# Layer 1: softplus summed on TensorE, 3x3 convolution on four 64x64 tiles; one output row per token in the mixture of experts

## The chip, the cores and the metric

One core of a Trainium2 chip runs the whole program. The time is the device time in microseconds (us), as the median of ten runs. Engines are named as in the profile: PE is TensorE, DVE is VectorE, ACT is ScalarE, POOL is GpSimd, SP is SyncE (it only issues DMAs here).

## The reference, cut to what matters

Input `x` is 32 images of 128 channels, 56x56, f32. Two layers follow each other.

Layer 0, a convolution block with a mixture of experts:

```python
x = conv7x7_depthwise(input); x = layernorm(x)           # T = 32*56*56 tokens of 128 values
topv, topi = top_k(x @ Wg, 2); wts = softmax(topv)       # two of E = 8 experts for each token
# each expert takes at most cap = 1.25*T/E tokens
h = gelu(einsum('ecd,edf->ecf', eb, W1) + b1)
y = einsum('ecf,efd->ecd', h, W2) + b2
moe = sum over the two experts of (gate * y)
return input + x + layer_scale * moe
```

Layer 1, a Mamba block beside a 3x3 depthwise convolution:

```python
xh = cv1_w @ x
l  = silu(batchnorm(conv3x3_depthwise(xh)))
t  = layernorm(xh)                                        # tokens in raster order
xm, z = split(t @ in_proj_w.T)                            # 256 channels each
xm = silu(causal_conv1d(xm, 4 taps))
dt, Bm, Cm = split(xm @ x_proj_w.T)
dt = softplus(dt @ dt_proj_w.T + dt_proj_b)
h_t = exp(dt_t * A) * h_(t-1) + dt_t * Bm_t * xm_t        # 16 states for each channel
y   = einsum(h_t, Cm_t) + xm * D
g   = (y * silu(z)) @ out_proj_w.T
out = x + cv2_w @ concat([l, g])
```

## The kernel before

The program runs in four stages, one after the other.

**Convolution** (to about 2000 us). The 7x7 depthwise convolution runs on PE; the normed tokens go to the DRAM tensor `res_d`, which has 2T rows of 128 values. Rows 0 to T-1 hold the tokens, rows T to 2T-1 are filled with zeros by 14 DMAs of 3584 KB (line 246). **Routing and dispatch** (to about 5025 us). DVE ranks the tokens; then POOL issues 1792 indirect DMAs that scatter token rows into `buf_d`, sorted by expert (line 404). Each row carries its gate and the index of the row of `res_d` that its result is to be added to: token t for the first choice of expert, T + t for the second (`backs`). **Experts** (to about 7054 us). For each expert, 35 groups of up to four tiles of 112 rows are loaded, multiplied on PE, and added to `res_d` by indirect DMAs with an add (`products`, line 455; 1120 of them, issued by POOL). `apart(inst, group)` declares that the DMAs of one group name don't depend on each other; all of them have the name "back".

**Layer 1** (to the end). A group is 8 rows of one image, 448 tokens; there are 32 x 7 = 224 groups, and each takes 16 steps, one for each state. The loop at the end of `layer1` writes the order of every engine's instructions out by hand (`manual_schedule`). Step t works on unit t, that is state i = t mod 16 of group g. In each step:

- ACT copies the last state of unit t-1 (`carry_act`, line 966), then computes exp(dt*A) of unit t+1 into the PSUM tile `da` (`exp_act`, two instructions, line 945; two `da` tiles).
- DVE does the scan of unit t (`scan_dve`, line 954) and the product with C (`cmul`, line 960). For the states 0, 3, 7, 11 and 14 (`POOL_C`) POOL does that product instead, a step later.
- POOL computes dt*B*xm of unit t+4 (`db_pool`, line 939).
- In odd steps PE adds the products of two units into the PSUM tile `py` (`sum_pe`, through `tiles`: four matmuls on the four 64x64 quarters of the array, line 902).
- Last come the side works, which the calls `at(offset, function)` put at step 16*g + offset: they prepare a later group or finish an earlier one. `yz_dve` alone comes ahead of the scan of its step.

In what follows "step 7" means all steps with t mod 16 = 7. Before the change the side works stand so: 14 `moe_act`; 6 `cv1_pe`; 7 `cv1_act`; 8 `var_pe`; 9 `rstd_act`; 10 `rstd_pool`; 11 `bc_pe`; 12 `te_dve`; 15 and 0 `xm_pe`; 1 `silus` (a table load, SiLU of the two halves of xm, of lt and of the two halves of z, with the z matmuls issued inside, and a table load back); 2 `px_pe`; 3 `px_act`; 4 `dt_pe`; 5 to 10 the softplus; 10 and 11 `lt_pe` (the 3x3 convolution: 9 matmuls with diagonal 128x128 weights); 12 `lt_act`; 2 `yz_dve`; 3 `out_pe`; 4 `out_act`; 13 `moe_pe` (two matmuls for each of four tiles, one for each half of `res_d`).

The softplus is computed as relu(v) + (ln(u) - ((u - 1) - e)) with e = exp(-|v|) and u = 1 + e. ACT does abs, relu, exp, the add of 1 and the logarithm; DVE does `sp_r` (line 856) and `sp_add` (line 868), POOL does `sp_sub` (line 864), each on 128x896 values.

All side works of PE share two PSUM banks through `mm_tile`: a new tile waits until the tile before the last one has been read.

Of the kernel before, what the change touches and what calls it, by code (L numbers as in the profile page):

```python
# [5 lines left out]
F32 = mybir.dt.float32  # L6
I32 = mybir.dt.int32
AF = mybir.ActivationFunctionType
ALU = mybir.AluOpType
# [34 lines left out]
def tile_kernel(tc: tile.TileContext, a: dict, out: bass.AP):  # L44
# [11 lines left out]
    with (  # L56
# [5 lines left out]

        res_d = dram.tile([2 * T, C], F32, name="res_d")


        zero = const.tile([TT, 1, RW], F32, name="zero")
        nc.gpsimd.memset(zero, 0.0)
        nc.gpsimd.memset(zero[:, :, C + 1].bitcast(I32), 2 * T)
        ident = const.tile([128, 128], F32, name="ident")
# [172 lines left out]
        for k in range(0, E * CAP // TT, 80):  # L242
            nc.sync.dma_start(out=buf_t[:, k : k + 80, :], in_=zero.to_broadcast([TT, 80, RW]))
        res_t = res_d.rearrange("(k p) c -> p k c", p=TT)
        for k in range(COLS, 2 * COLS, 64):
            nc.sync.dma_start(out=res_t[:, k : k + 64, :], in_=zero[:, :, :C].to_broadcast([TT, 64, C]))

# [140 lines left out]
        with tc.tile_pool(name="dispc", bufs=1) as dc, tc.tile_pool(name="disp", bufs=3) as dp:  # L388
            backs = []
            for k in range(2):  # L390
                bi = dc.tile([TT, COLS], I32, name=f"bi{k}")
                nc.gpsimd.iota(bi, pattern=[[TT, COLS]], base=k * T, channel_multiplier=1)
                backs.append(bi)
            for n in range(N):
                cols = slice(n * TPI, (n + 1) * TPI)
                for k in range(2):
                    xg = dp.tile([TT, TPI, RW], F32, name=f"xg{k}")
                    nc.sync.dma_start(
                        out=xg[:, :, :C], in_=res_d[n * L : (n + 1) * L, :].rearrange("(k p) c -> p k c", p=TT)
                    )  # L400
                    nc.vector.tensor_copy(xg[:, :, C], gates[k][:, cols])  # L401
                    nc.vector.tensor_copy(xg[:, :, C + 1].bitcast(I32), backs[k][:, cols])
                    for j in range(TPI):
                        apart(nc.gpsimd.indirect_dma_start(  # L404
                            out=buf_d[:, :],
                            out_offset=bass.IndirectOffsetOnAxis(
                                ap=slots[k][:, n * TPI + j : n * TPI + j + 1], axis=0
                            ),
                            in_=xg[:, j, :], in_offset=None, bounds_check=ZR - 1, oob_is_err=False,
                        ), "scatter")  # L410
# [4 lines left out]
        with (  # L415
# [12 lines left out]

            def products(g, xb, xc, w1t, w2t, b1t, b2t):

# [21 lines left out]
                )  # L452

                for j in range(g):
                    apart(nc.gpsimd.indirect_dma_start(  # L455
                        out=res_d[:, :],
                        out_offset=bass.IndirectOffsetOnAxis(ap=xb[:, j, C + 1 : C + 2].bitcast(I32), axis=0),
                        in_=ys[:, j, :], in_offset=None, bounds_check=2 * T - 1, oob_is_err=False, compute_op=ALU.add,
                    ), "back")

            for e in range(E):
# [10 lines left out]
                for i0 in range(0, ntile, GT):  # L472
# [11 lines left out]
                    if todo:  # L484
                        products(*todo.pop())
                    todo.append((g, xb, xc, w1t, w2t, b1t, b2t))
            products(*todo.pop())


        with (  # L490
# [36 lines left out]
            nc.vector.tensor_tensor(bbi, bbi, bsc, ALU.mult)  # L527
            nc.vector.tensor_tensor(bbi, bnb, bbi, ALU.subtract)

            wk = wp.tile([C, DC, DI], F32, name="wk")  # L530
# [99 lines left out]
def layer1(s):  # L630
# [5 lines left out]
    mm_tile, res_d, x_d, out_d = s["mm_tile"], s["res_d"], s["x_d"], s["out_d"]  # L636
    perm, T = s["perm"], s["T"]
    G = N * NQ1
# [4 lines left out]
    with (  # L643
# [23 lines left out]
        def fetch(g):  # L667
            n, q = divmod(g, NQ1)
            d = st[g]
            t0 = n * L + q * CH1  # L670
            d["x1"] = three.tile([C, CH1], F32, name="x1", bufs=5)
            nc.sync.dma_start(out=d["x1"], in_=x_d[n, :, q * CH1 : (q + 1) * CH1])
            d["yg"] = two.tile([TT, TPC1, 2, C], F32, name="yg")
            for k in range(2):
                r = k * T + t0
                nc.sync.dma_start(
                    out=d["yg"][:, :, k, :], in_=res_d[r : r + CH1, :].rearrange("(j p) c -> p j c", p=TT)
                )

        def moe_pe(g):  # L680
# [4 lines left out]
            for j in range(TPC1):  # L685
                for k in range(2):
                    nc.tensor.matmul(
                        p[:, j * TT : (j + 1) * TT], lhsT=yg[:, j, k, :], rhs=perm,
                        start=False, stop=k == 1 and j == TPC1 - 1,
                    )  # L690

# [144 lines left out]


        def sp_abs(g):
            d = st[g]
# [13 lines left out]

        def sp_r(g):
            d = st[g]
            nc.vector.scalar_tensor_tensor(d["e"], d["u"], 1.0, d["e"], ALU.subtract, ALU.subtract)

        def sp_ln(g):
            d = st[g]
            nc.scalar.activation(d["u"], d["u"], AF.Ln)  # L860

        def sp_sub(g):
            d = st[g]
            nc.gpsimd.tensor_tensor(d["u"], d["u"], d.pop("e"), ALU.subtract)

        def sp_add(g):
            d = st[g]
            nc.vector.tensor_tensor(d["dt"][:, :, 1:], d["dt"][:, :, 1:], d.pop("u"), ALU.add)

# [4 lines left out]

        def lt_pe(g, ts):
            d = st[g]
            if ts[0] == 0:
                d["p_l"] = mm_tile("p_l")
            for t in ts:
                dy, dx = divmod(t, 3)  # L880
                nc.tensor.matmul(  # L881
                    d["p_l"][:, :CH1], lhsT=s["dwd"][:, t, :], rhs=d["xh"][:, dy : dy + ROWS1, dx : dx + HW],
                    start=t == 0, stop=t == 8,
                )

        def lt_act(g):
            d = st[g]
            d["lt"] = two.tile([C, CH1], F32, name="lt")
            nc.scalar.activation(d["lt"], d.pop("p_l")[:, :CH1], AF.Identity, bias=s["bbi"], scale=s["bsc"])

# [89 lines left out]
        at(18, yz_dve)  # L980
        at(19, out_pe)
        at(20, out_act)
        at(-35, moe_pe)
# [5 lines left out]
        at(-22, rstd_pool)  # L989
        at(-21, bc_pe)  # L990
        at(-20, te_dve)
        at(-17, xm_pe, 0)
        at(-16, xm_pe, 1)
        at(-15, silus)
        at(-14, px_pe)
        at(-13, px_act)
        at(-12, dt_pe)
        at(-11, sp_abs)
        at(-10, sp_exp)
        at(-9, sp_r)  # L1000
        at(-8, sp_ln)
        at(-7, sp_sub)
        at(-6, sp_add)
        at(-5, du_pool)
        at(-6, lt_pe, range(0, 5))
        at(-5, lt_pe, range(5, 9))
        at(-4, lt_act)
        work.setdefault(DS * G - 15, []).append((silus, G))

# [76 lines left out]
```

## Time and profile before

| what | value |
|---|---|
| median of 10 runs | 18460.58 us (18454.04 to 18467.01) |
| the profiled execution | 18468.28 us, span 18466.6 us |
| convolution stage, to about | 2000 us |
| routing and dispatch, to about | 5025 us |
| experts, to about | 7054 us |
| layer 1 | 7054 us to the end |
| one group of layer 1 (scan of step 8 to the next: 12111.80 to 12162.29 us) | 50.49 us |

The profile's timeline gives for each instruction its start, its duration, the engine, the line of the kernel, the operation with output and inputs, and in brackets the idle time before it with what ended that. The duration of one instruction overlaps the next one on its engine by about 0.1 us, so sums along an engine are made with the distances of starts. One f32 matmul appears as two instructions (two passes), and so does its weight load.

### The profile page before, as it was taken

To read this page: it belongs to the slowest core of one execution; us is meant where nothing else is said; L and a number is where in the kernel's file an instruction comes from. 1 tells how busy PE (TensorE), PEld (TensorE's weight loads), DVE (VectorE), ACT (ScalarE), POOL (GpSimd) and SP (SyncE) were. 2 spreads that over 40 slices of the span, in tenths; PEclk is the share of its full clock that TensorE was granted. 3 is DMA by queue.
4 is the path that set the end of the run, shared out by engine and by line. 5 is a ranking of instruction groups with operands and counts; after the bars stand their busy time and mean duration, and the time that the engine had idled before them with its cause. 6 is when DMAs were issued, how large, how long until landed. Compare 5 with 4: busy or idle time off the path is not lost. (4 is left out here: it accounts for less than half of the span.)

```text
span 18466.6 us, 214770 instructions
## 1 busy us (share of the span) xinstructions
PE 13649.9 (74%) x75528; PEld 7238.3 (39%) x75528; DVE 12453.7 (67%) x9487; ACT 9674.8 (52%) x18556; POOL 14869.9 (81%) x9599
## 2 busy tenths in 40 slices
PE   4887110000099998888888888888888888888888
PEld 4887100000077774333333333333333333333333
DVE  1766730000011116999999999999999999999999
ACT  2333000000044445777777777777777777777776
POOL 1333036666688888999999999999999999999999
PEclk8997555555599999999999999999999999999999
DMA  9779622222255554555555555555555555555555
GB/s 224 205 208 203 146 57 66 66 68 68 52 67 68 68 67 118 166 166 165 166 164 165 165 164 165 166 165 165 166 164 164 165 165 165 166 166 166 165 165 155
DMA packets 1761563, 2633.97 MB, mean 143 GB/s; under 512 B 149674, under 2 KB 1220441, under 8 KB 1756385
## 3 DMA queue, kind: packets, MB, share of 16 engines
q1 hardware_dynamic: 1554656, 2464.60, 46.4%
q0 software_dynamic: 205824, 155.64, 5.9%
q8 instruction: 595, 9.75, 0.2%
q14 instruction: 488, 3.99, 0.1%
HBM read 2231.69 MB, written 426.81 MB: 144 GB/s over the span
## 5 line engine op out<-in xcount | busy, mean ns | idle before, releaser
L939 POOL TENSOR_TENSOR db<-du,bb 128x896 f32<-128x896 f32 x3584 | 7423.5, 2095 | 0.1
L954 DVE TENSOR_TENSOR_SCAN da<-da,db 128x898 f32<-128x898 f32 x2464 | 4978.2, 2020 | 86.8 <-ACT da L945 86.6
L945 ACT ACTIVATE da<-dt,aneg 128x449 f32<-128x449 f32 x7168 | 4578.4, 639 | 587.7 <-DVE hs L954 243.5
L902 PE MATMUL py<-prod,ident 64*64 64x448 f32 x28672 | 3475.1, 599 | 115.5 <-POOL prod L960 103.6
L960 DVE TENSOR_TENSOR prod<-da,cb 128x896 f32<-128x896 f32 x2464 | 2689.3, 1091 | 197.4 <-issue 4.4
L960 POOL TENSOR_TENSOR prod<-hs,cb 128x896 f32<-128x896 f32 x1120 | 2323.9, 2075 | 382.8 <-issue 329.6
L954 DVE TENSOR_TENSOR_SCAN hs<-da,db 128x898 f32<-128x898 f32 x1120 | 2262.1, 2020 | 246.7 <-ACT db L966 209.7
L404 POOL DMA_INDIRECT buf_d<-xg,slot x1792 | 1686.6, 941 | 816.5 <-issue 807.5
L481 PE MATMUL ept<-ident,xb 112*128 112x112 f32 x1120 | 200.0, 260 | 2530.9 <-DMA xb<-buf_d 2530.9
L483 ACT COPY xc<-ept 128x448 f32<-128x448 f32 x280 | 149.1, 532 | 3508.3 <-DMA xb<-buf_d 2531.0
L455 POOL DMA_INDIRECT res_d<-ys,xb x1120 | 1652.1, 1475 | 374.0 <-issue 323.4
L881 PE MATMUL p_l<-xh,dwd 128*128 128x448 f32 x4032 | 1745.9, 580 | 0.0
L902 PEld LDWEIGHTS py<-prod,ident 64*64 64x64 f32 x28672 | 982.7, 141 | 1942.2 <-issue 1115.6
L401 DVE COPY xg<-gate 112x28 f32<-112x28 f32 x64 | 13.5, 227 | 2252.6 <-DMA buf_d<-xg,slot 2252.5
L776 PE MATMUL p_xm<-te,wk 128*128 128x448 f32 x3584 | 1415.8, 546 | 0.0
L447 DVE TENSOR_TENSOR ys<-py,b2t 112x512 f32<-112x512 f32 x280 | 193.6, 691 | 1533.5 <-PE py L442 1525.9
L881 PEld LDWEIGHTS p_l<-xh,dwd 128*128 128x128 f32 x4032 | 793.4, 207 | 959.4 <-issue 958.0
L481 PEld LDWEIGHTS ept<-ident,xb 112*128 112x128 f32 x1120 | 137.5, 142 | 2532.0 <-issue 2531.8
L442 PEld LDWEIGHTS py<-w2t,hh 128*112 128x112 f32 x8960 | 1031.1, 177 | 163.4 <-issue 115.8
L442 PE MATMUL py<-w2t,hh 128*112 128x128 f32 x8960 | 1094.9, 275 | 0.0
L174 PE MATMUL pc<-xc,toep 112*112 112x112 f32 (+1 forms) x8192 | 980.3, 279 | 107.0 <-ACT toep L163 66.0
L203 POOL TENSOR_TENSOR xa<-xa,lng 112x896 f32<-112x896 f32 x128 | 278.6, 2176 | 955.2 <-DVE xa L200 602.6
(222 smaller groups left out, 19781.7 us busy)
## 6 DMA issues: line engine op xcount, KB each, us to landing
bb<-bc_d SPq DMA_DIRECT2D x1792, 448.0 KB
cb<-bc_d SPq DMA_DIRECT2D x1792, 448.0 KB
toep<-toep_d SPq DMA_DIRECT2D x448, 392.0 KB
xg<-res_d SPq DMA_DIRECT2D x64, 1568.0 KB
yg<-res_d SPq DMA_DIRECT2D x448, 224.0 KB
buf_d<-zero SPq DMA_DIRECT2D x14, 4550.0 KB
xb<-buf_d SPq DMA_DIRECT2D x280, 227.5 KB
xt<-in_x SPq DMA_DIRECT2D x32, 1568.0 KB
```

Source lines behind the costliest of these rows:

```text
L174: nc.tensor.matmul(pc[:, c, :, lo:hi], lhsT=tp[c // 2][:, c % 2, 6 - 2 * o : 8 - 2 * o, :], rhs=s4[:, c, :, lo + o - 1 : hi + o - 1], star ...
L404: apart(nc.gpsimd.indirect_dma_start(out=buf_d[:, :], out_offset=bass.IndirectOffsetOnAxis(ap=slots[k][:, n * TPI + j : n * TPI + j + 1], ...
L442: nc.tensor.matmul(py[:, j, :], lhsT=hh[:, k, j * TT : (j + 1) * TT], rhs=w2t[:, k, :], start=k == 0, stop=k == KF - 1,)
L455: apart(nc.gpsimd.indirect_dma_start(out=res_d[:, :], out_offset=bass.IndirectOffsetOnAxis(ap=xb[:, j, C + 1 : C + 2].bitcast(I32), axis=0 ...
L481: nc.tensor.transpose(pt[:, j * TT : (j + 1) * TT], xb[:, j, :C], ident[:TT, :TT])
L776: nc.tensor.matmul(p[:, :CH1], lhsT=s["wk"][:, k, hs], rhs=d["te"][:, k : k + CH1], start=k == 0, stop=k == DC - 1 and not first,)
L881: nc.tensor.matmul(d["p_l"][:, :CH1], lhsT=s["dwd"][:, t, :], rhs=d["xh"][:, dy : dy + ROWS1, dx : dx + HW], start=t == 0, stop=t == 8,)
L902: nc.tensor.matmul(st[g]["py"][h * HD : (h + 1) * HD, r, :CH1], lhsT=lhsT(rs, h), rhs=rhs[rs, h, :], start=start, stop=stop,)
L939: nc.gpsimd.tensor_tensor(dbv[i][:, :, 1:], st[g]["du"], units[u].pop("bb"), ALU.mult)
L945: nc.scalar.activation(da[:, h * W1 : (h + 1) * W1], st[g]["dt"][:, h, :], AF.Exp, scale=s["aneg"][:, h, i : i + 1])
L954: nc.vector.tensor_tensor_scan(hs, da, dbs[i], 0.0, ALU.mult, ALU.add)
L960: eng.tensor_tensor(w["prod"], w["hs"][:, :, 1:], w.pop("cb"), ALU.mult)
```

## The change

Four things change.

1. Both experts of a token add to the same row of `res_d`, which now has T rows: the 14 zero-fill DMAs go, the index of a row is t for both choices, and in layer 1 one DMA fetches a group's rows instead of two, with four matmuls instead of eight in `moe_pe`. The indirect DMAs of an expert have a group name of their own, so those of one expert wait for those of the experts before it.
2. The three elementwise steps of the softplus on DVE and POOL go. ACT now also subtracts 1 from u, four matmuls for each half (with the identity, or minus the identity for u - 1) add the four terms in PSUM, and ACT copies the two halves to `dt`.
3. The 3x3 convolution runs on the four 64x64 quarters of PE's array, as `sum_pe` does: a diagonal 128x128 weight needs only its two diagonal 64x64 blocks. For each tap there are four matmuls on 64 channels and 224 columns, into two PSUM tiles, and `lt_act` reads the result with four instructions on 64 x 224 values.
4. Most side works of layer 1 move by one or two steps.

```diff
-        res_d = dram.tile([2 * T, C], F32, name="res_d")
+        res_d = dram.tile([T, C], F32, name="res_d")
...
-        for k in range(COLS, 2 * COLS, 64):
-            nc.sync.dma_start(out=res_t[:, k : k + 64, :], in_=zero[:, :, :C].to_broadcast([TT, 64, C]))
...
-                    ), "back")
+                    ), f"back{e}")
...
+            bnt = wp.tile([128, 2, 2], F32, name="bnt")
+            for k in range(2):
+                for r in range(2):
+                    for j, v in enumerate((bbi, bsc)):
+                        nc.scalar.copy(bnt[k * HD : (k + 1) * HD, r, j : j + 1], v[r * HD : (r + 1) * HD, :])
+            negi = wp.tile([128, 128], F32, name="negi")
+            nc.vector.tensor_scalar_mul(negi, ident, -1.0)
...
-            for k in range(2):
-                r = k * T + t0
-                nc.sync.dma_start(
-                    out=d["yg"][:, :, k, :], in_=res_d[r : r + CH1, :].rearrange("(j p) c -> p j c", p=TT)
-                )
+            nc.sync.dma_start(
+                out=d["yg"], in_=res_d[t0 : t0 + CH1, :].rearrange("(j p) c -> p j c", p=TT)
+            )
...
-        def sp_r(g):
-            nc.vector.scalar_tensor_tensor(d["e"], d["u"], 1.0, d["e"], ALU.subtract, ALU.subtract)
         def sp_ln(g):
-            nc.scalar.activation(d["u"], d["u"], AF.Ln)
-        def sp_sub(g):
-            nc.gpsimd.tensor_tensor(d["u"], d["u"], d.pop("e"), ALU.subtract)
-        def sp_add(g):
-            nc.vector.tensor_tensor(d["dt"][:, :, 1:], d["dt"][:, :, 1:], d.pop("u"), ALU.add)
+            d["l"] = one.tile([128, 2, CH1], F32, name="sp_l")
+            nc.scalar.activation(d["l"], d["u"], AF.Ln)
+            nc.scalar.add(d["u"], d["u"], -1.0)
+        def sp_pe(g, h):
+            d[f"p_sp{h}"] = p = mm_tile("p_sp")
+            terms = ((s["negi"], d["u"]), (ident, d["e"]), (ident, d["l"]), (ident, d["dt"][:, :, 1:]))
+            for k, (w, v) in enumerate(terms):
+                nc.tensor.matmul(p[:, :CH1], lhsT=w, rhs=v[:, h, :], start=k == 0, stop=k == 3)
+        def sp_act(g, h):
+            nc.scalar.copy(d["dt"][:, h, 1:], d.pop(f"p_sp{h}")[:, :CH1])
...
         def lt_pe(g, ts):
-                d["p_l"] = mm_tile("p_l")
+                d["p_l"] = [mm_tile("p_l") for r in range(2)]
+            R = ROWS1 // 2
             for t in ts:
                 dy, dx = divmod(t, 3)
-                nc.tensor.matmul(
-                    d["p_l"][:, :CH1], lhsT=s["dwd"][:, t, :], rhs=d["xh"][:, dy : dy + ROWS1, dx : dx + HW],
-                    start=t == 0, stop=t == 8,
-                )
+                for r in range(2):
+                    rs = slice(r * HD, (r + 1) * HD)
+                    for k in range(2):
+                        nc.tensor.matmul(
+                            d["p_l"][r][k * HD : (k + 1) * HD, : CH1 // 2], lhsT=s["dwd"][rs, t, rs],
+                            rhs=d["xh"][rs, dy + k * R : dy + (k + 1) * R, dx : dx + HW], start=t == 0, stop=t == 8,
+                        )
         def lt_act(g):
-            nc.scalar.activation(d["lt"], d.pop("p_l")[:, :CH1], AF.Identity, bias=s["bbi"], scale=s["bsc"])
+            for r in range(2):
+                for k in range(2):
+                    nc.scalar.activation(
+                        lt[rs, k * CH1 // 2 : (k + 1) * CH1 // 2], ps[r][ks, : CH1 // 2], AF.Identity,
+                        bias=s["bnt"][ks, r, 0:1], scale=s["bnt"][ks, r, 1:2],
+                    )
...
-        at(19, out_pe)
-        at(20, out_act)
+        at(21, out_pe)
+        at(22, out_act)
...
-        at(-21, bc_pe), at(-20, te_dve), at(-17, xm_pe, 0), at(-16, xm_pe, 1), at(-15, silus)
-        at(-14, px_pe), at(-13, px_act), at(-12, dt_pe), at(-11, sp_abs), at(-10, sp_exp)
-        at(-9, sp_r), at(-8, sp_ln), at(-7, sp_sub), at(-6, sp_add), at(-5, du_pool)
-        at(-6, lt_pe, range(0, 5)), at(-5, lt_pe, range(5, 9)), at(-4, lt_act)
+        at(-20, bc_pe), at(-19, te_dve), at(-18, xm_pe, 0), at(-17, xm_pe, 1), at(-16, silus)
+        at(-15, px_pe), at(-14, px_act), at(-13, dt_pe), at(-12, sp_abs), at(-11, sp_exp)
+        at(-10, sp_ln), at(-9, sp_pe, 0), at(-8, sp_act, 0), at(-8, sp_pe, 1), at(-7, sp_act, 1)
+        at(-6, du_pool), at(-7, lt_pe, range(0, 5)), at(-6, lt_pe, range(5, 9)), at(-5, lt_act)
```

(The calls of `at` stand one to a line in the kernel.) After the change the side works stand so: 12 `bc_pe`; 13 `te_dve`, `moe_pe`; 14 and 15 `xm_pe`; 0 `silus`; 1 `px_pe`; 2 `px_act`, `yz_dve`; 3 `dt_pe`; 4 `sp_abs`; 5 `sp_exp`, `out_pe`; 6 `out_act`, `sp_ln`, `cv1_pe`; 7 `cv1_act`, `sp_pe` of half 0; 8 `var_pe`, `sp_act` of half 0, `sp_pe` of half 1; 9 `rstd_act`, `sp_act` of half 1, `lt_pe`; 10 `lt_pe`, `du_pool`; 11 `lt_act`.

## The prediction

> **What bounds the kernel now.** First the page, then the busy time of a stretch of layer 1, then the timeline of one group, engine by engine.
>
> ```profile
> span 18466.6 us, 214770 instructions
> 12000.00:13000.00 1000.00, 892.42 (x4514) 382.27 (x4513) 927.28 (x615) 720.00 (x1437) 962.38 (x560) 0.94 0.54 165
> ```
>
> The second line is from the windows (PE, PEld, DVE, ACT, POOL, granted clock, DMA share, GB/s). POOL and DVE look like the bound, PE is close behind. Who waits is seen in the timeline, DVE first:
>
> ```profile
> 12110.28 1.07 DVE L856 SCALAR_TENSOR_TENSOR sp_e<-sp_u,sp_e 128x896 f32<-128x896 f32 x1
> 12111.80 2.04 DVE L954 TENSOR_TENSOR_SCAN da<-da,db 128x898 f32<-128x898 f32 x1 [0.45 <-ACT da L945]
> 12121.19 1.08 DVE L868 TENSOR_TENSOR dt<-dt,sp_u 128x896 f32<-128x896 f32 x1
> 12142.36 1.09 DVE L894 TENSOR_TENSOR yz<-py,zs 128x896 f32<-128x896 f32 x1 [1.35 <-PE py L902]
> 12147.58 2.03 DVE L954 TENSOR_TENSOR_SCAN hs<-da,db 128x898 f32<-128x898 f32 x1 [1.07 <-ACT db L966]
> 12158.84 2.02 DVE L954 TENSOR_TENSOR_SCAN hs<-da,db 128x898 f32<-128x898 f32 x1
> ```
>
> DVE never waits for POOL. It waits 0.45 + 1.35 + 1.07 = 2.87 us a group, for ACT or PE; the other 50.49 - 2.87 = 47.62 us are its own work. POOL waits for DVE's scans (at 12110.50 below, 1.09 us after its last instruction), so DVE's chain sets the period, with POOL some 1.5 us behind it:
>
> ```profile
> 12110.50 2.64 POOL L960 TENSOR_TENSOR prod<-hs,cb 128x896 f32<-128x896 f32 x1 [1.09 <-issue]
> 12121.27 1.06 POOL L743 TENSOR_TENSOR rw<-r 112x4 f32<-112x4 f32 x1
> 12127.06 1.93 POOL L960 TENSOR_TENSOR prod<-hs,cb 128x896 f32<-128x896 f32 x1
> 12132.68 1.73 PE L902 MATMUL py<-prod,ident 64*64 64x448 f32 x16
> 12134.34 6.28 PE L776 MATMUL p_xm<-te,wk 128*128 128x448 f32 x16
> 12154.13 0.62 ACT L845 ACTIVATE sp_e<-p_dt,dtb 128x448 f32<-128x448 f32 x1
> 12160.89 1.31 ACT L945 ACTIVATE da<-dt,aneg 128x449 f32<-128x449 f32 x2 [1.26 <-DVE hs L954]
> 12162.14 0.62 ACT L706 ACTIVATE xh<-p_cv,cv1b 128x448 f32<-128x448 f32 x1
> ```
>
> Two things to see here. POOL's product takes 2.64 us beside `sp_r` and 1.93 us elsewhere, and its 112x4 step 1.06 us beside `sp_add` where its neighbours take 0.20: these two DVE steps also hold POOL up. And the exp of unit 8 (12160.89) starts when the scan of unit 7 ends (12158.84 + 2.02), so it uses that unit's `da`.
>
> **Layer 0.** The zero fill is issued from 1916 to 2113 us while DVE ranks the tokens until 2500 us, and DMA stands at 0 from 2150 us: it is hidden, removal gives 0. The seven new waits between experts stop POOL, with the next expert's DMAs behind it. The last indirect DMA starts at 7050.35 us and DVE is released by its landing at 7053.68, 3.33 us later; the next would have started after 1.76 us. So 1.57 us each, 11 us; POOL already waits 9.7 us there for `ys` in 6 places (waits, 5100 to 7000 us). Bounds 0 and 11 us, taken 4. The fetch of one half of `res_d` less saves SP 0.48 us and PE about 0.94 us a group, off the chain below.
>
> **What leaves DVE and POOL.** DVE loses `sp_r` and `sp_add`, 1.0 us each by distance of starts: 45.6 us of its own work are left. POOL loses `sp_sub` (2.05 us), 0.7 us of the product and 0.86 us of the small step: 3.6 us, so POOL falls further behind DVE's pace. The step lengths of DVE are then 3.13 us (scan and product), 1.93 us at states 0, 3, 7, 11, 14, plus 0.52 for `te_dve` in step 13 and 1.00 for `yz`. Everything now hangs on how long DVE waits for ACT and PE. Call S7 the start of the scan of step 7, and so on. There are three places.
>
> **1: `silus`, now in step 0.** ACT copies state 15 at S0 + 0.1, the exp of unit 1 ends at S0 + 1.56. Then table load 1.28, z matmuls 0.72 after it, both z halves read 2.44 after their matmuls began (12142.22 to 12144.66), table load 1.30: 5.74. Copy and exp of unit 2: 1.46 with the release, after 0.1. So S2 = S0 + 8.86. DVE's own work from S0 to S2 is 1.93 + 3.13 + 1.00 = 6.06. Wait: 2.80 us (before, with `silus` a step later, 1.35 + 1.07 = 2.42). PE is ready in time: `te` ends at S13 + 3.74, then 3.1 + 1.66 + 3.1 (half of p_xm, a pair of sums, the other half, from the rows above) to S13 + 11.85, against ACT's second SiLU at S13 + 12.07.
>
> **2: ACT from step 4 to 8.** ACT needs exp of unit 5 from S4 + 0.2 (1.25), `sp_abs` 2.07, copy and exp 1.45, `sp_exp` 1.82, copy and exp 1.45, `out_act` 0.52, ln 0.84, the new subtraction 0.86 (as the add of 1): S4 + 10.45. The scan of unit 7 ends at S4 + 11.4. If the exp of unit 8 waits for it as now, S8 = S4 + 11.44 + 1.40 = S4 + 12.84; DVE alone needs 3 x 3.13 + 1.93 = 11.32. Wait: 1.52 us. If it takes the other `da`, 0.73 us. I take the first: ACT is still behind the scan there, as in the row.
>
> **3: the new softplus on PE, and the convolution.** The first half's matmuls need a PSUM bank, which `cv1_act` frees: its first instruction starts at S8 - 0.15 and ends at S8 + 0.47. Then PE alone, in its order: half 0, 8 passes, 3.1 (as half of the 6.28 us row); `var_pe` 0.9; half 1, 3.1; a pair of sums 1.66; the convolution. The four quarters take 0.39 us for a set of 448 columns (four sets in 1.66 us with the switch), so 0.195 for 224, and 9 taps x 2 passes need 3.5, with the switch 3.6; above, if loading weights bounds it, 0.3 a set, 5.4. Sum: S8 + 12.88. Then `lt_act`: a row of 448 columns takes 725 ns and one of 4 columns 245, so 224 columns some 480, starts 0.36 apart: 1.45 for four (0.62 now). Behind it in ACT's queue wait copy and exp of unit 13: S13 = S8 + 15.95. DVE alone needs 14.45. Wait: 1.50 us. Before, this stretch had no wait: the convolution began without waiting for the softplus.
>
> The Trainium skill, page "TensorEngine Tiling (Array Packing)", section "PSUM Bottleneck", speaks against this part: tiling speeds up the matmuls, not the reading of PSUM, which can become the limit. By it the 3.4 us that PE saves in the convolution would count for nothing, and 0.83 us on ACT would be lost.
>
> **The sum.** Period 45.60 + 2.80 + 1.52 + 1.50 = 51.42 us against 50.49: +0.93, times 224 = +208 us. The first group's softplus is some 4 us longer, once (3.1 + 0.5 on PE and ACT for each half, and the subtraction, in place of 1.07 + 2.08 + 1.08), the waits between experts 4. From 18468 (the profiled execution) this gives 18684; it stood 8 us above the median, so 18675. With the other `da` the period is 50.63 and the time 18500; with 5.4 us for the convolution 53.2 and 19075.
>
> PE's clock is a further unknown. It fell from 1.00 to 0.50 after an idle time of 4.27 us (12108.57 to 12112.84), for 3.5 us. In the new order the longest gap is 3.2 us, before the sums of step 5: from 0 to about 0.5 us a group (the late `out_pe` delays `out_act`), at most 112 us. I take 0. The skill's page "TensorE: Matmul & The Clock Gate", section "Part 1: The HAM clock gate", has the clock fall after an idle window of about 3.4 us; by it this gap would just keep the clock.
>
> **The rivals.**
>
> *Faster: the PE chain is not late.* DVE waits at S13 only if `cv1_act` to `lt_act` takes more than 13.1 us on PE and ACT; the sum of place 3 has 14.6. If the identity matmuls and quarters overlap by 1.5 us more, or the scheduler gives half 0 its bank earlier, the wait of place 3 is 0; with 0.73 at place 2 the period is 45.60 + 2.80 + 0.73 = 49.13, -1.36, -305 us: 18165. For it: DVE and POOL do lose 2 and 3.6 us, and PE is only 89% busy. Against it: the matmuls of one bank follow each other in order, and the rows have them at 0.39 us a pass.
>
> *Much slower: place 3 is longer than that.* Weights of the quarters bound the convolution (5.4 us), or the clock falls: every us is a us of period. 19000 with the first.
>
> *The quarters don't run beside each other.* 72 passes of 0.195 one by one are 14 us: +10 us a group, over 20500. The row of `py` says otherwise: 16 passes of 448 columns in 1.73 us.
>
> **How the numbers follow.** Forecast 0.58 (own range 18480 to 18850), faster rival 0.25, much slower 0.14, one by one 0.03. About 0.2% (37 us) is what a measurement of this kernel can tell from no change; the forecast's low end lies inside that, which takes 0.07. So faster 0.25, same 0.07, slower 0.68. The range from 18150 to 18950 leaves out the last rival, half of the much slower one and the tail of the faster one.
>
> **What would show it.** Right: no DVE or POOL row for the softplus, POOL's product near 1.93 us everywhere; DVE about 45.6 us of work in a period of 51; its waits named ACT at the scans of steps 2, 8 and 13; ACT idle before `sp_act` and `lt_act` with PE as releaser; PE with hardly a gap from step 7 to 11. Wrong: a period under 50.3 with DVE busy through steps 9 to 13, or long waits at other steps, or the time found before 7054 us.

## The result, and the profile after

The changed kernel takes 18760.94 us (median of 8 runs, 18751.30 to 18771.79), the kernel before 18462.34 us (28 runs): a ratio of 1.0162, 95% interval 1.0153 to 1.0171, or +299 us. The profiled execution has a span of 18753.0 us against 18466.6.

The loss is in layer 1. The first scan starts at 7115.15 us instead of 7123.22, so all that stands before it gains 8 us. The distance from the scan of step 8 to the next such scan, as median over the groups, went from 50.50 to 51.88 us; the mean grew by 1.31 us, and 223 distances of that are 292 us.

Where in a group, the distances of DVE's scan starts tell (median over the groups, us; the column of step 1 is from the scan of step 1 to that of step 2). DVE alone needs 3.13 in a step with its own product, 1.93 where POOL has it (0, 3, 7, 11, 14), 4.13 with `yz`:

```
step      0    1    2    3    4    5    6    7    8    9    10   11   12   13   14   15
before    1.93 5.55 4.22 1.94 3.05 3.14 3.12 3.45 3.14 3.14 4.12 1.94 3.63 3.07 1.93 3.11
after     1.93 6.94 3.08 1.93 3.05 3.14 3.12 3.45 3.13 3.14 3.50 1.94 4.80 3.68 1.94 3.11
```

DVE waits 2.81 us in step 1, 1.52 in step 7, 0.37 in step 10 and 1.67 in step 12: 6.37 us where it waited 2.87 before. Its own work is 51.88 - 6.37 = 45.5 us. The busy time of the same stretch as before (PE, PEld, DVE, ACT, POOL, granted clock, DMA share, GB/s):

```profile
12000.00:13000.00 1000.00, 893.45 (x5598) 400.31 (x5590) 865.68 (x559) 764.77 (x1515) 870.02 (x525) 0.95 0.50 157
```

DVE and POOL are down to 87%, PE stays where it was: work was taken from the two busiest engines, and both now wait more than they gained. DVE's four waits in the timeline of one group (the one of step 1 has two parts, before `yz` and before the scan of step 2):

```profile
12234.01 2.04 DVE L969 TENSOR_TENSOR_SCAN da<-da,db 128x898 f32<-128x898 f32 x1 [1.43 <-ACT da L960]
12243.78 2.03 DVE L969 TENSOR_TENSOR_SCAN hs<-da,db 128x898 f32<-128x898 f32 x1 [0.29 <-ACT db L981]
12250.52 2.04 DVE L969 TENSOR_TENSOR_SCAN da<-da,db 128x898 f32<-128x898 f32 x1 [1.61 <-ACT da L960]
12266.37 1.09 DVE L909 TENSOR_TENSOR yz<-py,zs 128x896 f32<-128x896 f32 x1 [2.00 <-PE py L917]
12268.12 2.04 DVE L969 TENSOR_TENSOR_SCAN da<-da,db 128x898 f32<-128x898 f32 x1 [0.66 <-ACT db L981]
```

In order: the scans of steps 8, 11 and 13, then `yz` and the scan of step 2. What ACT does ahead of the third one, and PE ahead of ACT:

```profile
12237.84 0.53 ACT L870 COPY dt<-p_sp 128x448 f32<-128x448 f32 x1 [1.27 <-PE p_sp L866]
12241.73 0.53 ACT L870 COPY dt<-p_sp 128x448 f32<-128x448 f32 x1 [1.30 <-PE p_sp L866]
12246.80 2.19 ACT L901 ACTIVATE lt<-p_l,bnt 64x224 f32<-64x224 f32 x4 [1.69 <-PE p_l L888]
12249.12 1.30 ACT L960 ACTIVATE da<-dt,aneg 128x449 f32<-128x449 f32 x2
```

```profile
12240.78 0.92 PE L866 MATMUL p_sp<-dt,ident 128*128 128x448 f32 x2
12241.63 1.74 PE L917 MATMUL py<-prod,ident 64*64 64x448 f32 x16
12243.18 3.58 PE L888 MATMUL p_l<-xh,dwd 64*64 64x224 f32 x72
12246.59 1.68 PE L917 MATMUL py<-prod,ident 64*64 64x448 f32 x16
```

PE has no gap from the softplus to the end of the convolution (12243.18 + 3.58 = 12246.76). `lt_act` starts at 12246.80, ACT having stood idle for 1.69 us, and the exp of unit 13 stands behind it in ACT's queue. POOL's slow product and slow small step are gone together with `sp_r` and `sp_add`:

```profile
12232.71 1.93 POOL L975 TENSOR_TENSOR prod<-hs,cb 128x896 f32<-128x896 f32 x1 [1.11 <-PE py L917]
12240.72 0.20 POOL L743 TENSOR_TENSOR rw<-r 112x4 f32<-112x4 f32 x1
```

### The profile page after: what moved, and what is told of

The parts are those of the page before. It is cut to its first block, busy times and chain, and to the rows that moved or that the text cites. A ratio compares the mean times of both kernels' runs of the same rounds, so it can differ in the third digit from the quotient of the medians.

```text
span 18753.0 us, 243446 instructions
## 1 busy us (share of the span) xinstructions
PE 13895.8 (74%) x89416; PEld 7570.3 (40%) x89416; DVE 12042.2 (64%) x9040; ACT 10383.9 (55%) x19907; POOL 14077.2 (75%) x9374
## 5 line engine op out<-in xcount | busy, mean ns | idle before, releaser
L917 PE MATMUL py<-prod,ident 64*64 64x448 f32 x28672 | 3265.4, 566 | 550.2 <-POOL prod L975 543.1
L975 POOL TENSOR_TENSOR prod<-hs,cb 128x896 f32<-128x896 f32 x1120 | 2161.9, 1930 | 1320.9 <-PE py L917 805.6
L776 PE MATMUL p_xm<-te,wk 128*128 128x448 f32 x3584 | 1460.4, 550 | 354.1 <-DVE te L761 304.9
L776 PEld LDWEIGHTS p_xm<-te,wk 128*128 128x128 f32 x3584 | 642.7, 189 | 1045.5 <-issue 970.6
L174 PEld LDWEIGHTS pc<-xc,toep 112*112 112x112 f32 x8192 | 925.6, 193 | 114.1 <-ACT toep L163 69.6
```

Of the source, the lines that this page charges most:

```text
L174: nc.tensor.matmul(pc[:, c, :, lo:hi], lhsT=tp[c // 2][:, c % 2, 6 - 2 * o : 8 - 2 * o, :], rhs=s4[:, c, :, lo + o - 1 : hi + o - 1], star ...
L776: nc.tensor.matmul(p[:, :CH1], lhsT=s["wk"][:, k, hs], rhs=d["te"][:, k : k + CH1], start=k == 0, stop=k == DC - 1 and not first,)
L917: nc.tensor.matmul(st[g]["py"][h * HD : (h + 1) * HD, r, :CH1], lhsT=lhsT(rs, h), rhs=rhs[rs, h, :], start=start, stop=stop,)
L975: eng.tensor_tensor(w["prod"], w["hs"][:, :, 1:], w.pop("cb"), ALU.mult)
```

## The experiments

Two theories were to be told apart. A: the period is DVE's own work plus waits at three places, each set by a chain through ACT or PE; each edit is worth what it does to the chain that ends last there. The rivals: an engine's total amount of work (PE's, ACT's, POOL's) sets the period wherever the work stands. The runs were made on chips on which the kernel before took 18423, 18422, 18156 and 18162 us; every kernel is compared with runs of the kernel before on its own chip. In the profiles the first scan starts at 7069 to 7089 us on the first two chips and at 6806 to 6823 on the other two, against 7115 and 7123 above, so what differs between the chips lies ahead of layer 1. "Against the changed kernel" means that difference, less the 299 us above. No run takes part 2, the softplus, out of the changed kernel by itself.

**Part 1 alone.** The kernel before with the edits of part 1 and no others: `res_d` of T rows, no zero fill, one fetch, four matmuls in `moe_pe`, and a group name for each expert.

```diff
-                for k in range(2):
-                    nc.tensor.matmul(p[...], lhsT=yg[:, j, k, :], rhs=perm, ...)
+                nc.tensor.matmul(p[...], lhsT=yg[:, j, :], rhs=perm, ...)
```

> The kernel before with the first part of the change alone: both experts of a token add to one row, no zero fill of the second half, one fetch and four matmuls less in moe_pe. Theory A (DVE's waits for the chain of ACT and PE set the period of layer 1): PE and SP work saved in moe_pe and fetch is off the chain, so the period stays at 50.49 us; layer 0 gains what the two profiles show there, 24 us by the end of the convolution, less 6 us of waits between experts: 15 to 18 us less than before, 18445. Rival B (PE is so busy that its amount of work sets the period): 0.94 us less in each of 224 groups, some 210 us less, 18250. If the 24 us are chance of one profile: 6 us more, 18468.

Measured: 18221.91 us, ratio 0.9891 (0.9874 to 0.9907), -201 us. The period fell from 50.50 to 49.61 us, and all of it lies in step 1: 4.65 us instead of 5.55, every other step as before. So A's reading, that the fetch and `moe_pe` stand off the chain, falls: PE's 0.9 us count in this order. Why is seen in PE's timeline:

```profile
12035.45 1.02 PE L679 MATMUL p_moe<-x,ident 128*128 128x448 f32 x2
12036.31 1.04 PE L681 MATMUL p_moe<-perm,yg 112*128 112x112 f32 x8
12037.28 1.73 PE L895 MATMUL py<-prod,ident 64*64 64x448 f32 x16
12038.94 6.28 PE L769 MATMUL p_xm<-te,wk 128*128 128x448 f32 x16
12045.15 1.73 PE L895 MATMUL py<-prod,ident 64*64 64x448 f32 x16
```

There is no idle time in brackets from `moe_pe` to the sums that `yz` (12046.96) waits for: all that PE saves in this stretch comes off the wait at its end.

**The same part taken out of the changed kernel.** Two rows for each token, with the softplus, the convolution and the order as changed.

> The changed kernel with the two rows for each token of before (zero fill, two fetches, eight matmuls in moe_pe, one group name for all experts); softplus, convolution and order as changed. Alone, in the order of before, one row for each token was worth 0.9 us a group. Theory A (in the changed order PE stands idle 1.59 us between moe_pe and xm, waiting for te, so 0.87 us more of moe_pe is hidden): period 51.8 to 52.0, within 45 us of the changed kernel, so 1.014 to 1.019 of the kernel before. Rival B (PE's amount counts in every order): the wait before yz grows by 0.9, period 52.6 to 52.9, +170 to +210 us, 1.026 to 1.028 of the kernel before.

Measured: 18459.94 us against 18162.29, ratio 1.0163 (1.0150 to 1.0177), period 51.88: the same as the changed kernel. Here PE stands idle behind `moe_pe`, waiting for `te`, 0.69 us in this kernel and 1.59 in the changed one:

```profile
12060.34 1.02 PE L694 MATMUL p_moe<-x,ident 128*128 128x448 f32 x2
12061.19 1.94 PE L697 MATMUL p_moe<-perm,yg 112*128 112x112 f32 x16
12063.82 3.25 PE L786 MATMUL p_xm<-te,wk 128*128 128x448 f32 x8 [0.69 <-DVE te L771]
```

A holds. The same edit is worth 200 us in the old order and nothing in the new one. Set against part 1 alone, parts 2 to 4 therefore cost not 299 but 500 us.

**Place 3, `lt_act` later.** In the changed kernel `lt_act` is called first among the side works of step 12, so it stands behind the exp of unit 13 instead of ahead of it:

```diff
-        at(-5, lt_act)
+        at(-4, lt_act)
         at(-20, bc_pe)
```

> The changed kernel with lt_act one step later (step 12 instead of 11), behind the exp of unit 13 in ACT's queue. All else, PE's and ACT's work too, is the same. Theory A: the exp of unit 13 no longer waits for the convolution on PE, so the wait before the scan of step 13 (1.67 us) goes and only the 0.36 us before step 11 stay: some 1.7 us a group, 375 us, 18385. Rival B (the amount of PE's work, 89% busy and slowed by its clock, sets the period): no difference, 18760.

Measured: 18345.43 us, ratio 0.9958 (0.9941 to 0.9975), -376 us against the changed kernel: 0.4% faster than the kernel before. Step 12 is 3.11 us instead of 4.80, no other step changed; `lt_act` now runs in time in which ACT was waiting:

```profile
12047.18 1.30 ACT L960 ACTIVATE da<-dt,aneg 128x449 f32<-128x449 f32 x2
12048.42 2.17 ACT L901 ACTIVATE lt<-p_l,bnt 64x224 f32<-64x224 f32 x4
12050.81 1.31 ACT L960 ACTIVATE da<-dt,aneg 128x449 f32<-128x449 f32 x2
12053.33 0.16 ACT L981 COPY db<-da 128x2 f32<-128x2 f32 x1 [1.21 <-DVE prod L975]
```

**Place 2, `da` by turns.** In the changed kernel the exp of unit 8 can no longer take the tile of unit 7:

```diff
-            da = units[u]["da"] = pda.tile([128, 1024], F32, name="da")
+            da = units[u]["da"] = pda.tile([128, 1024], F32, name="da", tag=f"da{u % 2}", bufs=1)
```

> The changed kernel with the two da tiles bound to even and odd units, so that the exp of unit 8 takes the tile of unit 6 and not that of unit 7. Theory A: it starts when ACT is ready, not when the scan of unit 7 ends; ACT is ready 0.65 to 0.8 us earlier, the whole chain from cv1_act on moves by that: 145 to 180 us less, 18600. Rival B (PE's work): no difference, 18760.

Measured: 18582.68 us, ratio 1.0087 (1.0070 to 1.0104), -139 us against the changed kernel; step 7 is 2.82 us instead of 3.45, the period 51.26. The wait is where the prediction put it.

**ACT's amount.** The changed kernel without the subtraction on ACT; the 1 goes into the bias of the copies (`one_col` holds ones).

```diff
-            nc.scalar.add(d["u"], d["u"], -1.0)
...
-            nc.scalar.copy(d["dt"][:, h, 1:], d.pop(f"p_sp{h}")[:, :CH1])
+            nc.scalar.activation(d["dt"][:, h, 1:], d.pop(f"p_sp{h}")[:, :CH1], AF.Identity, bias=one_col)
```

> The changed kernel without the instruction of ACT that subtracts 1 from u; the two copies from PSUM add 1 instead (they become activations of some 0.62 us, from 0.53). The result differs from the changed kernel's in rounding alone. Theory A: the subtraction ends 0.65 us before the exp of unit 8 may start, which waits for the scan of unit 7; so taking away 0.86 us there gives nothing by itself: within 30 us of 18760. Rival C (ACT's amount of work counts): 0.7 us a group, 155 us less, 18605.

Measured: 18710.23 us, ratio 1.0155 (1.0138 to 1.0172), 12 us less than the changed kernel, inside the interval. 0.86 us of work a group less on ACT, of which the two copies take back 0.1 us each, is worth nothing: the exp of unit 8 waits for the scan of unit 7 anyway. The rival of ACT's amount falls.

**Part 3 taken out.** The changed kernel with `lt_pe` and `lt_act` as before the change.

```diff
-                for r in range(2): for k in range(2): nc.tensor.matmul(d["p_l"][r][...], lhsT=s["dwd"][rs, t, rs], ...)
+                nc.tensor.matmul(d["p_l"][:, :CH1], lhsT=s["dwd"][:, t, :], ...)
```

> The changed kernel with the 3x3 convolution and its one ACT instruction as before the change. In the changed kernel PE works without a gap from the softplus of step 8 to the convolution, and four ACT instructions follow that end. Theory A (this chain sets the wait of step 12): the convolution takes 18 passes of 0.39 us = 7.0 instead of 3.4, ACT 0.7 instead of 2.2, so step 12 is 2.1 us longer (4.8 to 6.9), the period 53.9 to 54.1 us, +440 to +500 us against the changed kernel. Rival B (what PE saves in the convolution goes into the reading of PSUM): within 60 us of the changed kernel, the period 51.6 to 52.1.

Measured: 19155.81 us, ratio 1.0399 (1.0383 to 1.0414), +435 us against the changed kernel, period 53.85, step 12 6.76 us: theory A, a little under its range. The convolution takes 7.03 us, and ACT waits 5.25 for it:

```profile
12037.18 0.72 ACT L891 ACTIVATE lt<-p_l,bbi,bsc 128x448 f32<-128x448 f32 x1 [5.25 <-PE p_l L883]
```

In the changed order the quarters are worth 1.97 us a group, about the 3.6 us of PE less the 1.5 of ACT. What the prediction weighed from the Trainium skill's page "TensorEngine Tiling (Array Packing)", section "PSUM Bottleneck", that tiling speeds up the matmuls and not the reading of PSUM, agrees with this in part: the reading went from 0.72 to 2.19 us, and that takes back less than half of the gain.

**Part 4 taken out.** All operations as changed, but most side works at the steps they had before (`bc_pe` and `te_dve` stay, `lt_act` stands as in the run with `lt_act` later).

```diff
-        at(21, out_pe), at(22, out_act), at(-18, xm_pe, 0), at(-17, xm_pe, 1), at(-16, silus), at(-15, px_pe), ...
+        at(19, out_pe), at(20, out_act), at(-17, xm_pe, 0), at(-16, xm_pe, 1), at(-15, silus), at(-14, px_pe), ...
-        at(-10, sp_ln), at(-9, sp_pe, 0), at(-8, sp_act, 0), at(-8, sp_pe, 1), at(-7, sp_act, 1)
+        at(-8, sp_ln), at(-8, sp_pe, 0), at(-7, sp_act, 0), at(-7, sp_pe, 1), at(-6, sp_act, 1)
```

> All operations of the change, but silus, xm, px, dt, the first steps of the softplus, out and lt_act stand at the steps they had before the change (bc and te stay one step later, lt_act is called first in step 12). Theory A (PE's chain from cv1 to yz sets the period): in the kernel with one row a token PE has no gap from 12018.3 to yz at 12047, scan of step 8 to yz 29.7 us; the softplus adds 6.2 us there and the quarters take off 3.6, so 32.3; then 1.0 + 4.2 to the scan of step 3 and 14.7 to the next step 8: period 52.0 to 52.4, from 0 to +120 us against the changed kernel, with a wait of 3.5 to 4.2 us before yz for PE. Rival B (the new places of the side works cause the loss; PE's chain has room): DVE's 45.6 us and the waits 0.45 + 1.5 + 1.1 of the kernel before: period 48.5 to 49.0, -640 to -760 us against the changed kernel, wait before yz under 1.5 us.

Measured: 19425.49 us, ratio 1.0545 (1.0529 to 1.0562), +705 us against the changed kernel, period 55.08. Both theories missed. The wait before `yz` is only 1.45 us in the median, but steps 10 and 11 last 5.12 and 4.72 us:

```profile
12023.18 0.53 ACT L870 COPY dt<-p_sp 128x448 f32<-128x448 f32 x1 [2.75 <-PE p_sp L866]
12028.05 0.53 ACT L870 COPY dt<-p_sp 128x448 f32<-128x448 f32 x1 [2.93 <-PE p_sp L866]
12028.53 1.33 ACT L960 ACTIVATE da<-dt,aneg 128x449 f32<-128x449 f32 x2
```

ACT's queue works in order: each copy of the softplus waits for its eight passes on PE, and the exp of the next unit waits behind the copy. PE's clock has a part in it: in this order PE idles 4.27 us ahead of `var_pe`, the granted clock falls to half, and the passes of half 0 take 4.9 us from first start to last end, those of half 1 3.3. The new order, in which the logarithm stands two steps and half 0 one step earlier, is worth 3.2 us a group to the changed kernel, and 4.9 against the run with `lt_act` later (50.18), which has `lt_act` at the same place. The two theories looked at PE's chain and at DVE's places; the trace puts the loss on the wait inside ACT's queue, as in place 3. How much of it is the clock and how much the later start was not separated.

**Part 3 in the old order.** The kernel with one row for each token, with the quarters, all nine taps in step 10, `lt_act` in step 11; the softplus stays on DVE and POOL.

```diff
-        at(-6, lt_pe, range(0, 5))
-        at(-5, lt_pe, range(5, 9))
-        at(-4, lt_act)
+        at(-6, lt_pe, range(0, 9))
+        at(-5, lt_act)              # called ahead of bc_pe
```

> The kernel before with one row for each token and with the convolution on four 64x64 quarters, all of it in step 10, lt_act (four instructions) in step 11; the softplus stays on DVE and POOL. Against the kernel with one row a token alone (period 49.6 us, PE without a gap from 12018 to 12047, waits of DVE 0.45 at step 8, 0.6 before yz, 1.1 before the scan of step 3). Theory A (ACT's silus hold the scan of step 3, ACT's new 1.5 us lie in its idle 1.4 + 2.8 us of steps 11 and 12): the wait before yz goes, the one behind it grows by as much, period 49.5 to 49.8, within 40 us. Rival B (reading PSUM in four instructions costs what PE saves): a wait of 0.8 to 1.5 us at step 12 or 13, +180 to +330 us. Rival C (PE's amount counts, as with the rows): 48.7 to 49.1, -120 to -200 us.

Measured: 18587.51 us, ratio 1.0090 (1.0076 to 1.0104): the period is 51.21, 1.60 us above that with one row alone. This has the size of rival B but not its place: all of it lies in step 1 (6.27 us instead of 4.65), none in 11 to 13. PE's timeline, and the windows over the same stretch (granted clock third from the end), show a cause that no theory had:

```profile
12054.72 0.98 PE L914 MATMUL py<-prod,ident 64*64 64x448 f32 x8
12058.75 1.77 PE L914 MATMUL py<-prod,ident 64*64 64x448 f32 x8 [3.04 <-POOL prod L972]
12060.45 1.84 PE L685 MATMUL p_moe<-x,ident 128*128 128x448 f32 x2
12062.10 1.07 PE L687 MATMUL p_moe<-perm,yg 112*128 112x112 f32 x8
```

```profile
12055.70:12058.70 3.00, 0.01 (x1) 0.00 (x0) 2.91 (x4) 1.81 (x4) 3.00 (x3) 1.00 0.46 153
12058.70:12060.50 1.80, 1.75 (x9) 0.36 (x9) 1.77 (x2) 0.00 (x0) 1.80 (x1) 0.51 0.37 139
```

With 3.6 us less to do PE idles 3.04 us for a product of POOL, its clock falls to half, and the sums and the first matmuls of `moe_pe`, just ahead of the chain to `yz`, take 1.6 us more (0.79 each), as much as the period grew.

**The gap filled.** The same kernel with `moe_pe` one step earlier, in that gap.

```diff
-        at(-35, moe_pe)
+        at(-36, moe_pe)             # called after bc_pe
```

> One row for each token and the convolution on quarters in step 10, lt_act in step 11, as in the run that came out at a period of 51.2 us; moe_pe now stands in step 12 instead of 13. In that run PE, with less to do, idled 3.04 us ahead of the sums of step 13, its granted clock fell to 0.5 for 3.5 us, and moe_pe took 3.2 instead of 1.8 us and the sums 1.8 instead of 1.0 just ahead of xm, the chain to yz. Theory A (the clock's fall is the whole loss of 1.6 us): no fall, as moe_pe fills the gap to 1.4 us; the wait before yz is 0.6 or less, period 49.4 to 49.7, 0.987 to 0.990 of the kernel before. Rival B (the four ACT instructions that read PSUM are the loss): the period stays 50.8 to 51.3, about 1.009.

Measured: 17928.15 us against 18155.67, ratio 0.9876 (0.9861 to 0.9891); the period is 49.61, the wait before `yz` is gone (step 1 is 4.11 us), and that of the scan of step 3 has grown (step 2 is 4.78). The scan of step 3 now waits for ACT, behind `silus`:

```profile
12081.09 2.03 DVE L966 TENSOR_TENSOR_SCAN hs<-da,db 128x898 f32<-128x898 f32 x1 [1.63 <-ACT db L978]
```

The time is that of A, and B falls: the four ACT instructions cost nothing in step 11 (1.94 us, as before). But the edit does two things: the clock falls at step 13 in 14 groups instead of 221, and `moe_pe` is out of the stretch ahead of `xm_pe`. PE starts `xm_pe` 3.2 us earlier behind the scan of step 8 (20.1 instead of 23.3 us, medians), about twice what the clock had cost, and ACT's chain hides the rest. That the fall of the clock was the whole loss therefore rests on the timeline of the run before, not on this run. The ratio is the lowest of all runs, but its interval overlaps with those of part 1 alone and of the last run below.

**Two edits together, then three.** First the changed kernel with `lt_act` later and `da` by turns.

> The changed kernel with lt_act first in step 12 and the two da tiles taken by turns: both single edits together. Theory A (the waits of steps 8 and 12 are separate and add up): period 50.18 - 0.63 = 49.5 to 49.6, -500 to -530 us against the changed kernel, so 0.987 to 0.989 of the kernel before. Rival B (PE's chain takes up what the first edit leaves): the wait of step 8 goes into a longer wait before yz, the period stays 50.0 to 50.2, 0.993 to 0.997 of the kernel before.

Measured: 18333.17 us, ratio 0.9954 (0.9940 to 0.9967), period 50.2 to 50.3: rival B's time, not its mechanism. Step 7 varies from group to group: about 2.8 us in 65 of 224, 3.9 in the median of the rest. The half clock lasts 3.41 us in the first and 6.83 us in the others, as in these two windows:

```profile
12026.84:12030.25 3.41, 3.41 (x11) 1.19 (x7) 3.31 (x3) 3.35 (x7) 3.41 (x2) 0.50 0.42 135
12125.82:12132.65 6.83, 6.15 (x14) 2.49 (x15) 6.60 (x6) 6.61 (x13) 6.83 (x5) 0.50 0.33 109
```

In the others `out_act` waits for `out_pe`, which runs behind a gap at half clock:

```profile
12126.50 1.77 PE L917 MATMUL py<-prod,ident 64*64 64x448 f32 x8 [2.37 <-POOL prod L975]
12128.21 1.86 PE L930 MATMUL p_out<-x,ident 128*128 128x448 f32 x2
12129.86 1.70 PE L931 MATMUL p_out<-lt,cvlt 128*128 128x448 f32 x2
12131.35 2.31 PE L934 MATMUL p_out<-yz,wo 128*128 128x448 f32 x4
```

```profile
12133.70 0.63 ACT L939 ACTIVATE ot<-p_out,cv2b 128x448 f32<-128x448 f32 x1 [1.11 <-PE p_out L934]
```

Then a third edit on top of these two:

```diff
-        at(21, out_pe)
-        at(22, out_act)
+        at(19, out_pe)
+        at(20, out_act)
```

> The changed kernel with lt_act first in step 12, da tiles by turns, and out_pe and out_act at the steps 3 and 4 they had before the change. With only the first two edits step 7 was 2.82 us in 29% of the groups and 3.4 to 4.0 in the rest: PE idles 2.37 us ahead of the sums of step 5, its clock falls to half, out_pe takes up to 5.2 us instead of 3.3 and out_act waits for it up to 1.1 us, with the logarithm and two exps queued behind. Theory A (that fall costs the 0.65 us): step 7 is 2.82 in nearly all groups, period 49.5 to 49.7, 0.987 to 0.989 of the kernel before. Rival B (the wait of step 12, once gone, comes back at step 7 whatever the clock does): period 50.1 to 50.3. Rival C (the second half of dt_pe now waits for out_act's PSUM bank): a new wait at step 4 or 5 of 0.5 to 1.5 us, period over 50.

Measured: 18289.11 us against 18155.67, ratio 1.0074 (1.0060 to 1.0088), period 51.22. Half of A came true: step 7 is 2.99 us in nearly all groups. The second half of `dt_pe` does wait for `out_act` (rival C), but only 0.77 us and without a wait of DVE behind it. What made the kernel slower is that PE's idle time went elsewhere: PE now idles 4.66 us ahead of the first half of the softplus, whose eight passes take 4.6 us instead of 3.1, and steps 9 and 10 grow by 1.1 and 0.4:

```profile
12015.81 1.86 PE L866 MATMUL p_sp<-sp_u,negi 128*128 128x448 f32 x2 [4.66 <-ACT xh L706]
12017.46 1.60 PE L866 MATMUL p_sp<-sp_e,ident 128*128 128x448 f32 x2
```

**A floor.** The kernel before with one row for each token and `da` by turns.

> The kernel before with one row for each token, and with the two da tiles taken by turns, so that the exp of unit 8 need not wait for the scan of unit 7. Theory A (the waits of DVE add up: 0.45 of the period of 49.6 us goes): period 49.1 to 49.3, -75 to -105 us against the kernel with one row a token, ratio to the kernel before 0.983 to 0.985. Rival B (PE's chain to yz takes it up: var_pe follows cv1_act, which follows that exp): if cv1_act starts earlier too, PE's chain starts earlier as well and A holds; if it doesn't, the 0.45 go into the wait before yz: 49.6, ratio 0.989.

Measured: 17953.35 us against 18155.67, ratio 0.9889 (0.9874 to 0.9905), period 49.59. Neither theory: step 7 lost 0.53 us, and step 10 gained as much, where `sp_add`, beside POOL's work, took 1.60 us instead of 1.08. Three kernels with the old softplus, with different waits of DVE, all stand at 49.6; in each POOL is busy for 977 to 980 of 1000 us, with one idle time of about 0.7 us a group. POOL's amount may be the floor of these three; that was not tested by taking work from POOL alone. A rival for one of them stands above: in the kernel with `moe_pe` earlier the wait that left `yz` is back before the scan of step 3, where ACT ends it (1.63 us instead of 1.08), so there ACT's chain explains the unchanged period without POOL.

## Why the prediction was right

The sign, the place and the size hold: 18675 forecast, 18761 measured, and layer 1 gave +292 us where the sum had +208. By its steps:

- **DVE's own work**: 45.6 forecast, 45.5 measured. POOL's rows fell to 1.93 and 0.20 us as said. The three places took back more than that: DVE waits 6.37 us where it waited 2.87.
- **Place 1**: 2.80 forecast, 2.81 measured. ACT and PE are nearly level there: PE waits 0.33 us for ACT's SiLU before the z matmuls. DVE's scans of steps 2, 8 and 13 wait for ACT, as the prediction's signs had it; they did not have the wait before `yz`, 2.00 of the 2.81 us, which PE ends, nor the 0.37 us at the scan of step 11. Dropping the saving of the fetch and `moe_pe` was right for the order as changed (the run with two rows), but the reason given was not general: in the order of before that saving is on the path to `yz`, 0.9 us a group. The prediction had read that wait of 1.35 us for PE and not followed PE's chain back through `moe_pe`.
- **Place 2**: 1.52 forecast and measured. The other `da` tile gives 0.63 us less where the prediction had 0.79.
- **Place 3**: 1.50 forecast, 1.67 + 0.37 measured. The term that was mis-sized is `lt_act`: 1.45 us forecast, 2.2 measured. Each of its four instructions lasts 534 ns, not 480, and starts 0.55 us after the last, not 0.36: these four don't overlap, where other neighbours on ACT do by 0.1 us. The convolution was 3.4 us (forecast 3.6), the quarters do run beside each other, and its start at S8 + 9.17 was forecast at S8 + 9.23. These 0.54 us are 120 us of the kernel. Against them stand 0.1 us less of DVE's own work (22 us), all that comes before the first scan (16 us) and a mean of the periods that grew by 0.07 less than the median (16 us): together most of the 71 us by which the profiled execution, 18754.76 us, lies above the 18684 of the sum. That three small errors took off nearly half of the large one is luck.
- **Before the first scan**: +4 us forecast for the waits between experts, +4 for the first group's softplus and 0 for the zero fill; measured -8 in all. The waits between experts cost 6 us, the stretch from the last indirect DMA to the first scan grew by 4, and the stretch of routing and dispatch between, for which the sum had no term, by another 6. The step that failed is "it is hidden, removal gives 0": the convolution stage, in whose last stretch those DMAs are issued, ends 24 us earlier without them (its last logits are written at 1942.5 instead of 1966.4 us), half of it in that stretch; the other half stands before the first of them is issued at 1916 us, so it is not theirs. That they are the cause of the rest was not tried by itself; the changed kernel with two rows ended the stage at 1923 us, kernels with one row, on other chips, at 1907 to 1916.
- **PE's clock**: taken 0, and in the changed kernel it costs next to nothing (step 7 is 3.48 in the mean and 3.45 in the median). The expected gap of 3.2 us is 2.37, and the clock does fall behind it, so the prediction's reading of the 3.4 us, by which such a gap just keeps the clock, did not hold.

```profile
12221.10:12223.40 2.30, 0.00 (x0) 0.00 (x0) 2.27 (x3) 2.00 (x5) 1.94 (x2) 1.00 0.12 42
12223.40:12227.60 4.20, 4.16 (x13) 1.82 (x14) 4.10 (x4) 4.10 (x8) 4.20 (x3) 0.62 0.30 109
```

It is hidden because the exp of unit 8 waits for a scan anyway; with `lt_act` later and `da` by turns it shows, in step 7. The four quarters ran beside each other (3.4 us for 72 passes), so that rival fell. The faster one needed place 3 not to be late; the run with `lt_act` behind the exp shows how close it was, one place in ACT's queue.

## What to carry to other kernels

Work taken from the busiest engines was worth nothing here, where another engine's chain ended last; first find, for each wait, the stretch in which the releasing engine has no idle time, since only what stands in that stretch counts. In a queue that works in order, put an instruction that waits for another engine behind those on which the critical engine depends: one such move turned this change from 1.6% slower to 0.4% faster. And an edit's price belongs to an order of work: the single row was worth 200 us in the old order and nothing in the new one.

## What the runs showed of the hardware that I had not expected

Less work on PE can make it slower. A gap of 2.37 us was enough to halve the granted clock, for 3.41 or 6.83 us, where one of 1.70 us in the same kernel (ahead of the softplus) was not; 3.04 us cost 1.6 us a group, and moving the gap elsewhere moved the loss (4.66 us ahead of the softplus, 1.5 us). The Trainium skill, page "TensorE: Matmul & The Clock Gate", section "Part 1: The HAM clock gate", has the fall after an idle window of about 3.4 us that runs freely. The gap here is shorter than that; that the half clock lasts 3.41 us in some groups and 6.83 in others at a fixed gap agrees with windows of that length that run freely.

An ACT instruction that reads 64 x 224 values from PSUM took 534 ns, one on 128 x 448 values 720 (`lt_act` of before): half the columns, and a quarter of the values, for three quarters of the time.
